# A four-layer graph attention stack: new start, new end and new ranks in the planned order

## Chip, cores and metric

The kernel runs on one core of one Trainium2 chip. The metric is the device time of one execution in microseconds, as a median of runs. Everything is in 32-bit floating point.

## What is computed

`x` has 128 graphs of 64 nodes with 512 features; `adj` is one 64 x 64 mask for each graph. Four pre-norm layers add to `x`; each one starts with `h = relu(layernorm(x))`.

```
layers 0, 2: q, k, v = h@Wq, h@Wk, h@Wv            # 4 heads of 64
             p = softmax(where(adj, q@k.T / 8, -max));   x += (p@v)@Wo + bo
layer 1:     g = layernorm(h)*gamma + beta;  q, k, v = g@Wqkv.T   # 8 heads of 64
             p = softmax(where(adj or eye, q@k.T / 8, -1e9));  x += (p@v)@w_out.T + b_out
layer 3:     m = h@map_w.T + map_b;  n = m / |m| by head          # 8 heads of 64
             q = m@q_w.T + q_b;  k = m@k_w.T + k_b
             p = softmax(where(mask, -1e10, q@k.T / 8)) * keep
             a = (n@n.T > 0.1) * p
             x += relu((a @ (h@gcn_map_w.T + gcn_map_b)) @ gcn_W.T / (sum(a) + 1))
```

## The kernel before

The 8192 rows of `x` are cut into 16 groups of 512 rows, which are four blocks of 128, two graphs to a block. The names used below are `(l, s)` for layer and group. A group goes through a layer in these steps: load (`loads`), layer norm (`layernorms`, one stream for each half of 256 rows), transposition of the tokens (`transposes`), projections (`projections`), scores and softmax (`front`), transposition of the probabilities (`turns`), and PV, output projection and residual (`attention`; `last` in layer 3).

**Products.** A projection is a 2 x 2 block product. `winograd` does it with seven half-size products instead of eight, into banks named `mA`, `mB` and `mC`. It needs sums of the weights (`sums_of_a`, once for each weight) and of the transposed tokens (`sums_of_b`, four for each operand, into a tile `t` and, for the third, in place). GpSimd makes most of these sums; for group 0 of layer 0 VectorE makes them. ScalarE and VectorE then take the results out of the banks. V of layers 0 and 2 has half the width. Scores, PV and the last transposes are 64 x 64 matmuls.

**Transposition of the tokens.** The first groups of layers 0 and 2 go through TensorE (`ptr`, L672), each block of 128 rows evicted by one ScalarE copy (L676). The others of these layers are moved by 16 DMAs of 32 rows each (`moves`, L630) into `F`, and VectorE then transposes 32 x 32 blocks (L645). In layers 1 and 3 ScalarE and GpSimd make the moves.

**The order of the work.** The order on every engine is written out by a planner in the kernel (`Order`): each stream of work is a generator that yields operations with an assumed cost (`pe(0.432)`, `act(0.6)`, `load(3.9)`). At each step the planner issues the operation that can start first by its own clock; among equals the lower rank wins. The table `RANK` gives a rank for each kind of stream and layer. Evictions have rank 0 and may go ahead of others on ScalarE and VectorE. On the chip each engine then runs its list in this order and waits where it must. SyncE (SP) issues nearly all DMAs, also in this order.

**The start.** SP issues four loads of one block each for group 0. ScalarE issues the first weights, Wq and Wk of layer 0, in four parts, and then the two loads of group 1. SP goes on with the mask, Wv and Wo. `x` has two buffers (`r_xin`).

**The end.** In layer 3 the residual rows of two blocks are loaded into one of three buffers (`r_xres`, L1279), VectorE adds the clamped PV to it (`finish`, L1293), and SP stores it (L1298). The softmax of layer 3 is multiplied by the neighbour mask, its sums are made, and `divide` divides by them on GpSimd (L1080). The last group's probabilities are transposed by TensorE (`by_tensor`, L1106), not by copies. `add_rows` (L954) adds a bias row to V on GpSimd, four instructions a group, after V has been evicted.

Of the kernel before, what the change touches and what calls it, by code (L numbers as in the profile page):

```python
# [14 lines left out]
P = 128  # L15
D = 512
N = 64
TB = 4
NC = D // P
# [11 lines left out]

RANK = {
    "load": (6.5, 0.3, 3, 3.5),
    "norm0": (4.5, 5.5, 6, 5.5),
    "norm1": (4.5, 6, 5, 6),
    "move": (6.5, 6.5, 2, 6.5),
    "turn": (3, 1.5, 4.5, 3.5),
    "part": (4, 1.5, 5, 5),
    "weight": (0.3, 6.5, 0.3, 3),
    "proj": (3.5, 5, 5, 6),  # L40
    "out": (1.5, 5, 5, 0.3),
    "front": (2, 3.5, 0.5, 4),
    "soft": (0.3, 3, 1, 4.5),
    "near": (3, 0.5, 6, 4),
    "trans": (4, 3.5, 3, 2.5),
    "att": (2.5, 2.5, 2, 6),
    "res": (2.5, 2.5, 4.5, 4.5),
    "msum": (1, 4, 1, 1),
    "length": (5, 5, 0.3, 5),
# [195 lines left out]
def gnn_stack(ctx: ExitStack, tc: tile.TileContext, a: dict, out: bass.AP):  # L245
# [109 lines left out]
    first_w, first_t, begun_w, loads_begun = (od.event() for _ in range(4))  # L355
    bo, bo_done = {}, {}

    def sums_of_a(A, vector=False):

        for o, i0, i1, op in ((4, 2, 3, ALU.add), (5, 4, 0, ALU.subtract),  # L360
                              (6, 1, 5, ALU.subtract), (2, 0, 2, ALU.subtract)):
            if vector:
                yield dve(0.75)
                nc.vector.tensor_tensor(A[:, o], A[:, i0], A[:, i1], op)
            else:
                yield pool(0.0026 * A.shape[2] * A.shape[3])
                nc.gpsimd.tensor_tensor(A[:, o], A[:, i0], A[:, i1], op)

    def sums_of_b(B, T, made, vector=False):

        for i, o, i0, i1 in ((0, T[0], B(0, 1), B(0, 0)), (1, T[1], B(1, 1), T[0]),
                             (2, T[2], B(1, 1), B(0, 1)), (3, T[3], B(1, 0), T[1])):
            if vector:
# [5 lines left out]
            if i:  # L379
                made[i].set()  # L380

# [3 lines left out]
    def weights():  # L385
        for key, parts in units:
# [5 lines left out]
            first = key == "qk0"  # L392
            for src, dst in parts(t):
# [8 lines left out]
            if first:  # L402
                begun_w.set()
                yield ("wait", 0.0, 5.0)
                first_w.set()
                yield ("wait", 0.0, 2.5)
                yield loads_begun
# [17 lines left out]
            yield from sums_of_a(t, key == "qk0")  # L425
            w_sums[key].set()

# [42 lines left out]
    def scales(v, there=None):  # L470

        mv = small.tile([P, 2, 2], F32, tag="mv", name="mv")
        for t in range(2):
# [4 lines left out]
            nc.vector.bn_stats(st, v[:, t, :])  # L478
            yield dve(0.17)
# [41 lines left out]
    def loads(steps):  # L521
        for l, s in steps:
# [3 lines left out]
            for half in range(2):  # L526
# [5 lines left out]
                if (l, s) == (0, 1):  # L532
                    if half == 0:
                        yield begun_w
                    yield ("act", 0.5, 0.0)
                elif (l, s) == (0, 0):
# [11 lines left out]
                (nc.scalar if (l, s) == (0, 1) else nc.sync).dma_start(  # L548
                    v, x_of(l, s)[half * H:(half + 1) * H, :].rearrange("(t p) d -> p t d", p=P))
                if (l, s) == (0, 1):  # L550
                    if half == 1:
                        loads_begun.set()
                    yield ("wait", 0.0, 8.0)
# [4 lines left out]
    def layernorms(steps, half):  # L558

        for l, s in steps:  # L560
            yield rank(f"norm{half}", l) if (l, s) != (0, 0) else Rank(0.3)
# [3 lines left out]
            rs = yield from scales(x, first_x[2 * half:] if (l, s) == (0, 0) else None)  # L565
# [84 lines left out]
    def transposes(steps):  # L650

        for l, s in steps:
            yield rank("turn", l) if (l, s) != (0, 0) else Rank(0.3)
# [9 lines left out]
            for half in range(0 if (l, s) in turned + by_dma else 2):  # L663
                yield n_ready[l, s, half]
                x, xe = normed[l, s]
                for t in range(2):
                    b = 2 * half + t
                    pt, pe_ = yield from r_mm.new("ptr")
                    pt = pt.rearrange("p (c n) -> p c n", c=NC)
                    for c in range(NC):  # L670
                        yield pe(0.115)
                        nc.tensor.transpose(pt[:, c, :], x[:, b, c * P:(c + 1) * P], ident)  # L672
                    if b == TB - 1:
                        xe.set()
                    yield act(0.6)
                    nc.scalar.copy(h[:, :, b * P:(b + 1) * P], pt)  # L676
                    pe_.set()
                if (l, s, half) == (0, 0, 0):
                    yield from has_h(l, s, h)
            if (l, s) != (0, 0) and (l, s) not in turned:  # L680
                yield from has_h(l, s, h)
            yield from sums_of_b(quarters(h), *hB[l, s][1:], (l, s) == (0, 0))
            if (l, s) == (0, 0):
                first_t.set()

    def has_h(l, s, h):
        T, t_done[l, s] = yield from r_t.new("T")
        hB[l, s] = (quarters(h), with_room(T, quarters(h)), made())
# [822 lines left out]
```

## Time and profile before

| | us |
|---|---|
| median of 3 runs | 2678.46 (2673.72 to 2681.55) |
| profiled execution | 2677.01 |
| its span | 2675.2 |
| TensorE busy in it | 2630.3 |
| VectorE, ScalarE, GpSimd busy | 1853.5, 1889.7, 1591.0 |
| granted TensorE clock, mean | 0.998 |

The table of busy times tells which engine has no room left. The table by stage divides the span and shows where TensorE is idle. The list of waits tells for what. The timeline shows the instructions in order of time, with start, duration, and in brackets the idle time before with what ended it. Times of one profiled execution are used throughout; they are spans from the first instruction to the last, so the execution's own time is a little longer.

### The profile page before, as it was taken

The numbers are of one execution on the slowest core, as the hardware profiler recorded it, in microseconds if no ns is written. First come the engines' busy times: TensorE is split into PE (matmuls) and PEld (weight loads), VectorE is DVE, ScalarE is ACT, GpSimd is POOL, SyncE is SP. The second block draws the span as 40 slices with busy tenths as digits, with TensorE's granted clock in tenths as the row PEclk, the third lists the DMA queues.
The fourth block names the chain that finished last, engine by engine and source line by source line (L and its number), as shares of the span: only waits on it lengthen the run. The fifth ranks groups of instructions, "written<-read, shape, count | busy, mean of one in ns | idle before, by whom it ended". The sixth has DMA issues, their size and how long they took to land.

```text
span 2675.2 us, 63987 instructions
## 1 busy us (share of the span) xinstructions
PE 2630.3 (98%) x26344; PEld 2308.6 (86%) x26344; DVE 1853.5 (69%) x2842; ACT 1889.7 (71%) x3517; POOL 1591.0 (59%) x1248
## 2 busy tenths in 40 slices
PE   7999999999999999999999999999999999999998
PEld 6888888888888888888899999988888888888887
DVE  6777676677667766766667777757676667776566
ACT  5676767888887788787567777776667766677653
POOL 4776776645444543545666767786556555556553
PEclk9999999999999999999999999999999999999999
DMA  5665663212111211114556666422322232222222
GB/s 155 165 178 141 171 150 129 85 65 80 49 49 65 80 49 59 68 66 104 138 155 155 166 151 170 141 76 81 94 66 66 81 101 78 66 65 70 68 82 59
DMA packets 413940, 270.02 MB, mean 101 GB/s; under 512 B 277456, under 2 KB 322512, under 8 KB 413648
## 3 DMA queue, kind: packets, MB, share of 16 engines
q1 hardware_dynamic: 401440, 253.35, 34.3%
q10 hardware_dynamic: 12208, 12.58, 1.4%
q8 instruction: 207, 3.39, 0.5%
q14 instruction: 85, 0.70, 0.1%
HBM read 166.77 MB, written 67.63 MB: 88 GB/s over the span
## 4 chain that ended last, share of the span: by engine, by line
PE 91%; DMA 2%; DVE 2%; SPq 2%; ACT 1%; issue 1%; POOL 1%; DVEq 0%; ACTq 0%; POOLq 0%
PE mA L714 47%; PE mC L714 23%; PE mB L714 12%; PE sc L1038 3%; PE po L1240 2%; PE cos L1038 1%; PE po L1410 1%; SPq L630 1%; PE mmn L981 1%; DMA F<-xin 1%; DMA w_vo<-in_Wv 0%; ACT E L1060 0%; SPq L548 0%; DMA adj<-in_adj 0%; DMA w_k<-in_Wk 0%
## 5 line engine op out<-in xcount | busy, mean ns | idle before, releaser
L1177 POOL TENSOR_TENSOR xres<-xres,u 128x512 f32<-128x512 f32 x192 | 247.5, 1295 | 415.7 <-ACT u L1172 389.6
L1089 ACT COPY F<-E 32x512 f32<-32x512 f32 x752 | 462.6, 615 | 23.3 <-POOL E L1080 12.4
L494 ACT ACTIVATE xin<-xin,rs 128x512 f32<-128x512 f32 x320 | 244.1, 808 | 36.0 <-DMA F<-xin 18.4
L1156 POOL TENSOR_TENSOR xres<-xres,u 128x512 f32<-128x512 f32 x192 | 252.9, 1335 | 25.6 <-DMA xres<-in_x 13.8
L594 ACT COPY hT<-xin 32x512 f32<-32x512 f32 x390 | 240.1, 616 | 7.2
L478 DVE BATCH_NORM_STATS2 st<-xin 128x6 f32<-128x512 f32 x320 | 213.8, 668 | 29.5 <-DMA xin<-in_x 19.4
L731 ACT COPY v<-mA 128x256 f32<-128x256 f32 (+1 forms) x192 | 92.1, 479 | 136.5 <-PE mA L714 133.4
L378 POOL TENSOR_TENSOR t<-hT,t 128x512 f32<-128x512 f32 x126 | 184.4, 1463 | 4.8 <-issue 1.5
L485 POOL TENSOR_TENSOR rs<-rs,mhalf 128x2 f32<-128x2 f32 x160 | 117.4, 737 | 71.8 <-DVE rs L483 48.2
L1074 DVE TENSOR_REDUCE sm<-E 128x16 f32<-128x1024 f32 x124 | 150.1, 1211 | 9.1 <-ACT E L1060 4.6
L714 PE MATMUL mA<-w_vo,t 128*128 128x128 f32 (+1 forms) x768 | 141.3, 316 | 4.1 <-ACT v L731 2.6
L378 POOL TENSOR_TENSOR t<-hT 128x512 f32<-128x512 f32 x63 | 92.9, 1475 | 79.7 <-DVE hT L604 54.8
L1080 POOL TENSOR_TENSOR E<-E,sm 128x1024 f32<-128x1024 f32 x64 | 122.0, 1916 | 25.9 <-DVE sm L1078 21.1
L1172 ACT COPY u<-mA 128x512 f32<-128x512 f32 x144 | 84.3, 586 | 74.2 <-PE mA L714 71.6
L714 PE MATMUL mA<-hT,w_qk 128*128 128x256 f32 x512 | 132.5, 385 | 4.3 <-ACT v L731 4.2
L731 ACT COPY qk<-mA 128x512 f32<-128x512 f32 x96 | 56.2, 585 | 111.2 <-PE mA L714 107.9
L591 POOL COPY hT<-xin 32x512 f32<-32x512 f32 x90 | 55.7, 618 | 131.3 <-ACT xin L494 128.8
L714 PEld LDWEIGHTS mA<-w_vo,t 128*128 128x128 f32 x768 | 115.0, 192 | 15.9 <-ACT v L731 2.8
L1093 DVE STREAM_TRANSPOSE F<-F 128x1024 f32<-128x1024 f32 x94 | 116.0, 1234 | 17.6 <-ACT F L1089 17.6
L954 POOL TENSOR_TENSOR v<-v,gcn_row 128x512 f32<-128x512 f32 x64 | 80.8, 1294 | 79.0 <-ACT v L731 79.0
L714 PE MATMUL mA<-t,w_qk 128*128 128x256 f32 x512 | 121.7, 380 | 5.5 <-POOL t L378 3.2
L1060 ACT ACTIVATE E<-sc,mx 128x64 f32<-128x64 f32 x512 | 122.4, 329 | 4.2 <-DVE mx L1057 4.2
(231 smaller groups left out, 7310.9 us busy)
## 6 DMA issues: line engine op xcount, KB each, us to landing
x<-xres SPq DMA_DIRECT2D x96, 512.0 KB
xin<-x SPq DMA_DIRECT2D x96, 512.0 KB
xres<-x SPq DMA_DIRECT2D x64, 512.0 KB
F<-xin SPq DMA_DIRECT2D x480, 64.0 KB
xres<-in_x SPq DMA_DIRECT2D x32, 512.0 KB
u<-rs SPq DMA_DIRECT2D x128, 128.0 KB
xres<-x SPq DMA_DIRECT2D x64, 256.0 KB
out<-xres SPq DMA_DIRECT2D x64, 256.0 KB
```

The costliest lines, as they stand in the source:

```text
L378: nc.gpsimd.tensor_tensor(o, i0, i1, ALU.subtract)
L478: nc.vector.bn_stats(st, v[:, t, :])
L494: nc.scalar.activation(v[:, t, :], v[:, t, :], func, bias=rs[:, 2, t:t + 1], scale=rs[:, 0, t:t + 1])
L594: nc.scalar.copy(o, v)
L714: nc.tensor.matmul(o, l, r, start=(first and m == 0 and k == 0), stop=(k == KC - 1), skip_group_check=True)
L731: nc.scalar.copy(o, p3)
L1060: nc.scalar.activation(E[:, i, :], S3[:, i, :], AF.Exp, bias=mx[:, i:i + 1], scale=0.125)
L1074: nc.vector.tensor_reduce(o, E, AX.X, ALU.add)
L1080: nc.gpsimd.tensor_mul(E, E, sm[:, :, None].to_broadcast([P, 16, N]))
L1089: nc.scalar.copy(F[g * N + 32 * k:g * N + 32 * (k + 1), :, 32 * i:32 * (i + 1)], E[g * N + 32 * i:g * N + 32 * (i + 1), :, 32 * k:32 * (k ...
L1156: nc.gpsimd.tensor_add(xr[:, t, :], xr[:, t, :], bo[l])
L1177: nc.gpsimd.tensor_add(v, v, both(u))
```

## The change

- **Start.** SP issues group 1's loads, ahead of Wv and Wo. VectorE writes a few elements into the buffers of both, once the statistics of group 0's last block have been issued, and the loads wait for these writes. `LEAD` names groups 0 and 1, and a rank `lead` holds for their layer norm and transposes. Two blocks of transposes share one bank pair and one ScalarE copy of twice the size (`from_bank`); this holds wherever TensorE transposes.
- **Group 0's Q and K.** `school` takes eight plain products instead of the seven of `winograd`: four with the first half of the tokens, four with the second. They need no sums. The sums of Q's and K's weights, which group 1 uses, are made once group 0 has been transposed; its own tokens' sums are still made, for V, the two that matter here (T[2] in place, and A[2] of the weights) only after the last of the eight products has read its operand.
- **End.** For the last group `divide` does its multiplication on VectorE. `finish` is started before PV and takes each of its two blocks as soon as that block's PV is done; in the last group it stores each block by itself, with half as many rows to a store and twice as many stores.
- **Ranks.** All ranks are new, and the planner's cost of one transpose step of the last group is 0.52 instead of 0.25.

```diff
+LEAD = [(0, 0), (0, 1)]
 RANK = {
-    "load": (6.5, 0.3, 3, 3.5),
-    "norm0": (4.5, 5.5, 6, 5.5),
-    "norm1": (4.5, 6, 5, 6),
-    "move": (6.5, 6.5, 2, 6.5),
...
-    "att": (2.5, 2.5, 2, 6),
-    "res": (2.5, 2.5, 4.5, 4.5),
...
+    "lead": (0.3, 1.5, 5.5, 5),
+    "load": (4, 5.5, 1.5, 2),
+    "norm0": (1.5, 3.5, 3.5, 6.5),
+    "norm1": (4.5, 2.5, 1, 4),
+    "move": (6.5, 4.5, 6, 0.3),
...
+    "att": (2.5, 0.5, 2, 2),
+    "res": (5.5, 6, 1.5, 5.5),
...
@@ def weights():
+            if key == "vo0":
+                yield x_there
+                yield dve(0.06)
+                nc.vector.memset(t.rearrange("p a k n -> p (a k n)")[:, 0:11 * H:2 * H], 0.0)
...
-                yield loads_begun
...
+            if first:
+                od.spawn(first_sums(t), rank("weight", 0))
+                continue
...
+    def first_sums(t):
+        yield h_whole
+        yield from sums_of_a(t, True)
+        w_sums["qk0"].set()
@@ def scales(v, there=None):
             nc.vector.bn_stats(st, v[:, t, :])
+            if there and there[t] is first_x[-1]:
+                x_there.set()
@@ def loads(steps):
-                if (l, s) == (0, 1):
-                    if half == 0:
-                        yield begun_w
-                    yield ("act", 0.5, 0.0)
+                if (l, s) == (0, 1) and half == 0:
+                    yield x_there
+                    yield dve(0.06)
+                    nc.vector.memset(x[:, :, 0:1], 0.0)
...
-                (nc.scalar if (l, s) == (0, 1) else nc.sync).dma_start(
+                nc.sync.dma_start(
@@ def transposes(steps):
-                for t in range(2):
-                    b = 2 * half + t
-                    pt, pe_ = yield from r_mm.new("ptr")
+                pt, pe_ = yield from r_sc.new("ptr")
...
+                od.spawn(from_bank(h[:, :, half * H:(half + 1) * H].rearrange(
+                    "p c (t n) -> p t c n", t=2), pt, pe_, copied), 0)
...
+    def from_bank(o, p_, pe_, done):
+        yield act(1.06)
+        nc.scalar.copy(o, p_)
+        pe_.set()
+        done.set()
...
+    def school(A, B, out_, used, begun, whole):
+        every = []
+        for k in range(2):
+            if k:
+                yield whole
+            room = []
+            for i in range(2):
+                room.append((yield from (r_mm if i else r_ma).new("mP")))
+            for j in range(2):
+                for i in range(2):
+                    yield from product(room[i][0], A[:, 2 * i + j], B(j, k), False, j == 0)
+                    if j:
+                        read, done = od.event(), od.event()
+                        od.spawn(out_.first(i, k, room[i][0], read, done), 0)
+                        od.spawn(when([read], room[i][1]), 0)
+                        every.append(done)
+                if k and not j:
+                    half_used.set()
+        begun.set()
+        od.spawn(when(every, used), 0)
@@
-    def divide(E, sm):
+    def divide(E, sm, vector=False):
...
-        yield pool(1.95)
-        nc.gpsimd.tensor_mul(E, E, sm[:, :, None].to_broadcast([P, 16, N]))
+        if vector:
+            yield dve(1.22)
+        else:
+            yield pool(1.95)
+        (nc.vector if vector else nc.gpsimd).tensor_mul(E, E, sm[:, :, None].to_broadcast([P, 16, N]))
@@ def by_tensor(E, e):
-                yield quads(0.25)
+                yield quads(0.52)
@@
-    def finish(s, u, po, poe, got):
+    def finish(s, u, po, poe, got, halves):
...
+            yield halves[b]
...
+            if s == NG - 1:
+                for s2 in range(2):
+                    yield load(2.8)
+                    q = slice(s2 * H, (s2 + 1) * H)
+                    o = out[(s * TB + 2 * u + b) * P:(s * TB + 2 * u + b + 1) * P, q]
+                    nc.sync.dma_start(o.rearrange("(i n) e -> n i e", n=N),
+                                      v[s2 * N:(s2 + 1) * N])
```

## The prediction

> **What bounds the kernel now.** I read the busy table first, then the table by stage, then who waited for whom, then the timeline at both ends.
>
> ```profile
> PE 2630.3 (98%) x26344; PEld 2308.6 (86%) x26344; DVE 1853.5 (69%) x2842; ACT 1889.7 (71%) x3517; POOL 1591.0 (59%) x1248
> ...
> 0.00:20.00 20.00, 8.60 (x29) 6.85 (x30) 9.68 (x33) 6.71 (x10) 6.67 (x15) 1.00 0.75 228
> 20.00:50.00 30.00, 24.52 (x206) 21.81 (x205) 19.75 (x45) 18.95 (x44) 10.24 (x11) 1.00 0.32 110
> 50.00:100.00 50.00, 46.10 (x483) 39.89 (x482) 35.04 (x52) 28.90 (x60) 40.69 (x33) 0.97 0.75 177
> 100.00:700.00 600.00, 592.93 (x5738) 528.82 (x5738) 426.81 (x722) 450.50 (x886) 377.48 (x308) 1.00 0.45 120
> 700.00:1350.00 650.00, 648.06 (x5855) 568.60 (x5853) 444.86 (x671) 487.91 (x766) 332.42 (x276) 1.00 0.26 78
> ```
>
> TensorE is busy for 2630.3 of 2675.2 us; nothing that leaves its work alone can win more than the other 45. The first two numbers of a stage are its length and PE's busy time. Of the 45 idle us, 11.4 lie in the first 20, 5.5 in the next 30, 3.9 in the next 50, 7.1 up to 700; all of 700 to 2660 has 6.3, and the last stretch after 2660 has 10.8. So there are three places to win: the start, layer 0, the tail.
>
> ```profile
> PE ptr L672 <- ACT xin L494: 11.3, 2, 8.9
> PE mA L714 <- ACT v L731: 7.8, 9, 2.6
> PE mA L714 <- DVE t L375: 3.2, 4, 2.3
> PE mA L714 <- POOL t L378: 3.2, 1, 3.2
> ```
>
> These waits (total, times, longest) name them: layer norm before the first transposes, evictions of V in layer 0, and the operand sums of groups 0 and 1. The timeline of the start and of the tail, start and duration first:
>
> ```profile
> 11.51 0.41 ACTq L548 DMA_DIRECT2D xin<-in_x  x1
> 11.95 0.58 ACT L676 COPY hT<-ptr 128x512 f32<-128x512 f32 x1 [2.43 <-DMA w_vo<-in_Wv]
> 14.48 2.93 PE L714 MATMUL mA<-hT,w_qk 128*128 128x256 f32 x6
> ...
> 2655.91 4.95 POOL L954 TENSOR_TENSOR v<-v,gcn_row 128x512 f32<-128x512 f32 x4 [5.12 <-ACT v L731]
> 2660.82 1.89 POOL L1080 TENSOR_TENSOR xin<-xin,f 128x1024 f32<-128x1024 f32 x1
> 2663.07 1.26 SPq L1279 DMA_DIRECT2D xres<-x  x2
> 2668.86 1.29 DVE L1293 SCALAR_TENSOR_TENSOR xres<-po,xres 128x512 f32<-128x512 f32 x2 [3.61 <-DMA xres<-x]
> ```
>
> ScalarE's first eviction of a transpose stands behind its own issue of group 1's second load. At the end the last residual load can go only when a store has freed its buffer, and the last VectorE step waits for that load.
>
> A third reading uses the start times of the mB product of each group's Q and K. In layer 2 it recurs every 26.62 us (1399.51, 1426.13, 1452.74); in layer 0 12 groups from 107.76 to 437.67 take 27.49 each. The work is the same. I add it from rows: a full product 1.73 x 7, V's product 0.89 x 7, the output's 0.86 x 7, scores and PV 1.01 each, four changes of tile size at 0.1: 26.8, so layer 2 runs without stalls and layer 0 loses 0.88 a group.
>
> **What the Trainium skill says.** "TensorE: Matmul & The Clock Gate", Part 1: the array runs at half clock until some 3.4 us of sustained work. The trace agrees: the 6 matmuls at 14.48 take 2.93 us where 8 take 1.89 later, and the rate is full from about 18.5. "DMA: Bandwidth & Descriptors", Anatomy of one DMA: a semaphore wait happens on the issuing sequencer, not in the DMA engine. The trace agrees: ACT had ended at 9.53 and stood until 11.51 with the issue at L548. The first page also has ScalarE and VectorE as strict FIFO (Architectural detail); the DVE load wait below bears it out, since everything behind it stood.
>
> **The change part by part.** The comparison is with the profiled execution's own 2677.0 us (span 2675.2 and 1.8 around it); the median of the runs shown, 2678.5, is 1.5 above it, so I add 1.5 at the end.
>
> *Start.* Group 1's two loads leave ACT's queue; SP issues them, and Wv and Wo, only after VectorE's memsets at about 9.4. Two memsets are added, 0.1 each by the row at 0.84. Eviction: transposes of blocks 0 and 1 end near 10.4, then one copy of two blocks (1.06 by the row of L1109, where two took 0.58 each). The first product starts at about 11.6 instead of 14.48. It is cold: 3.5; two cold transposes 1.6; so 16.7, then seven warm products 12.1 and one pair of group 1's transposes 0.9: Q and K end at 29.7. Before they ended at 33.0. This includes the eighth product, +1.73, which is paid; in return no product waits for T on VectorE (2.3) or for an eviction of its own bank. V and scores take 8.2 as before, so group 1 starts at about 37.9 (41.3 before). Its third product needs POOL's sums of group 1: their source is evicted by about 32.5, two sums at 1.3 end near 35, PE asks at 41.3, so the 3.15 wait goes. What is late next: group 2's transposed input, by 16 moves behind the layer norm at about 41.4, 0.85 each, some 2.5 to land and 2.5 on VectorE: 61 against a PE that could ask at 60. At 61 PE has done 46.7 us of work; before, at 74.0, it had done 49.2 and 1.73 less was due. So 74.0 - 61 - (49.2 - 46.7) - 1.73 = 8.8 net. The added wait: behind x_there on SP stand adj, bo, the vectors and group 2's loads; 2 MB at the 228 GB/s of the first stage are 8.8 us, so Wv lands near 19 to 20 and POOL's sums of it end by 26, where V wants them past 30. If the held loads took 10 us more, that cover would be gone and the gain with it. Bounds: -11 to -3; I take -8.8.
>
> *Layer 0 by the new ranks.* The order of instructions shows a pattern that repeats each group: V's seven products in a row, PV and output among the next group's Q and K. I walk one group with the durations above, S the end of scores. PV to S+1.0, three matmuls of mC to S+2.3, the PV copy (1.02) S+1.2 to 2.3: met. Exponentials in five bursts end at S+9.2, sum, reciprocal and POOL's division at S+13.2; the three F copies then run to S+15.1, the V eviction (0.37) to S+15.5, and PE wants its bank at S+15.8. The other V evictions are ready 0.2 to 0.8 early. The next hT is written by S+32.9 for S+33.3. SP: 16 moves at 0.75 to 0.85 end near S+24, plus 2.5 to land, for VectorE at S+30. So no stall, 26.8 a group; POOL has 19.4 of it. If all holds, 14 groups at 0.88 give 12. Margins of 0.2 to 0.4 us will not all hold; I take -7, bounds -13 to +4.
>
> *Layers 1 to 3 by the ranks.* PE's order is the same word for word over most of layer 1, and little changed in layers 2 and 3, which have almost nothing to win. The planner's costs are the old ones but for one, 0.52 for a group of the last transposes, which is what the trace has (64 in 2.08, in four groups). Its plans kept PE at 99.7% here from 700 on. A miss costs: +1.5, bounds -4 to +8.
>
> *Tail.* The division moves to VectorE: E times a factor at 1.23 (the L1374 row at 2651.05; the one at 2644.45 took 2.12) for POOL's 1.90, and the second one no longer stands behind 4.95 of row additions. PV of group 14 goes ahead of the last two V products, so its stores go 3.3 us earlier, the last residual load lands at 2665.4 instead of 2668.7. But these PV (2.1) and a transpose (2.1) now stand ahead of V's last product: its eviction, and POOL's four additions behind it, end 4 us later, at 2665. The last PV ends at 2665.5 (2667.1 before), the last half on VectorE at 2667.5 (2670.2). SP then issues eight stores of half the size instead of four, 0.6 each; its queue ends near 2670, 1.4 before the old end. I take -2, bounds -5 to +1.
>
> Sum: -8.8 - 7 + 1.5 - 2 = -16.3; 2677.0 - 16.3 + 1.5 = 2662.
>
> **Rivals.** *Only the ends win:* layer 0's stalls are placed anew, not removed. For it: every margin found is under half a microsecond. Against it: layer 2's pattern has no stall at all with the same work. -8.8 - 2 + 1.5: 2669. *The held loads come late:* VectorE's queue has two statistics of group 1 ahead of the sums of group 0's operands; were those loads to land 5 us later than the 14 to 16 reckoned, V of group 0 stands, and the start gains 3: with half of layer 0, 2672. Against it: before, such a load took 5 us with more traffic. *Slower: POOL or the moves become layer 0's clock.* In the new order SP's stores wait for POOL's last addition of the group, and the next half load and residual stand behind them; moves of the next group follow. The chain has 26.8 us and I find some 4 us of slack. If an issue takes 1.1 us instead of 0.75 to 0.95, 16 cost 4 to 5 more, the slack is gone, and each 0.1 beyond costs 1.6 a group: at 1.2, 1.6 in each of 14 groups, +22 in place of -7: 2692. Against it: issues in the stages shown are 0.6 to 0.95. *The change does less than it says:* the memsets could fail to hold the loads; but the SP instruction waits for a VectorE semaphore, so it holds.
>
> **How the numbers follow.** The forecast 0.55, only the ends 0.21, late loads 0.12, the slower case 0.12. A measurement of this kernel can tell about 0.3%, 8 us, from no change: faster is below 2670.5. The forecast's own range is 2653 to 2670; the first rival falls below 2670.5 for the most part. Faster 0.74, within 0.14, slower 0.12. With the bounds of the terms the range is 2652 to 2680; it leaves out the slower case and little else.
>
> **What would show it.** The first Q and K product at 11 to 12 us and Q and K done by 30; no wait of group 1 for POOL's sums; mB of Q and K in layer 0 every 26.7 to 27.0 us; layer 2 still at 26.6; the last residual load landed by 2666 counted on the old clock, the end 4 to 8 us after the last PV. Wrong would be a layer-0 spacing of 27.5 or more, V of group 0 waiting for a DMA, or new waits of over 1 us in layers 1 to 3.

## Result and the profile after

The changed kernel takes 2678.01 us (median of 13 runs, 2674.79 to 2685.52); the kernel before, on the same chip, 2678.3 (13 runs). The ratio is 1.0004, 95% interval 0.9995 to 1.0014: no difference, where 2662 was forecast.

The busy table of the changed kernel, then its table by stage (stage, length, PE's busy time, then PEld, VectorE, ScalarE, GpSimd):

```profile
PE 2629.7 (98%) x26352; PEld 2308.0 (86%) x26352; DVE 1918.9 (72%) x2843; ACT 1890.3 (71%) x3508; POOL 1608.8 (60%) x1246
```

```profile
0.00:20.00 20.00, 10.08 (x37) 8.50 (x38) 8.27 (x32) 6.24 (x7) 2.12 (x8) 1.00 0.73 240
20.00:50.00 30.00, 29.92 (x233) 27.02 (x232) 25.01 (x51) 21.17 (x45) 21.59 (x21) 1.00 0.41 125
50.00:100.00 50.00, 46.86 (x499) 42.16 (x498) 35.92 (x55) 31.94 (x71) 38.44 (x31) 0.97 0.69 162
100.00:700.00 600.00, 597.49 (x5769) 532.07 (x5768) 465.56 (x732) 455.95 (x882) 383.57 (x315) 1.00 0.45 123
700.00:1350.00 650.00, 648.36 (x5941) 569.06 (x5940) 459.44 (x676) 487.79 (x785) 322.00 (x275) 1.00 0.26 78
1350.00:2000.00 650.00, 647.09 (x6407) 574.74 (x6406) 461.02 (x713) 459.67 (x947) 463.22 (x344) 1.00 0.46 122
2000.00:2500.00 500.00, 487.38 (x5441) 416.14 (x5440) 350.84 (x456) 337.94 (x613) 298.09 (x209) 1.00 0.30 76
```

The kernel before has, in its last two of these stages:

```profile
1350.00:2000.00 650.00, 649.52 (x6499) 575.26 (x6498) 465.10 (x717) 455.39 (x955) 446.11 (x344) 1.00 0.46 125
2000.00:2500.00 500.00, 497.25 (x5417) 427.35 (x5418) 340.95 (x471) 350.59 (x634) 294.39 (x213) 1.00 0.27 76
```

TensorE's idle time is length minus busy, and the whole span then adds up:

| stage, us | idle before | idle after | difference |
|---|---|---|---|
| 0 to 100 | 20.8 | 13.1 | -7.7 |
| 100 to 700 | 7.1 | 2.5 | -4.6 |
| 700 to 1350 | 1.9 | 1.6 | -0.3 |
| 1350 to 2000 | 0.5 | 2.9 | +2.4 |
| 2000 to 2500 | 2.7 | 12.6 | +9.9 |
| 2500 to the end | 11.9 | 10.5 | -1.4 |
| PE busy, all | 2630.3 | 2629.7 | -0.6 |
| span | 2675.2 | 2673.0 | -2.2 |

The start and layer 0 win 12.3 us of idle time, and the stages from 1350 to 2500, which end in layer 3, give 12.3 back.

Idle time is only part of it, since the same work can keep TensorE busy for longer or shorter. A better measure is a point at which both kernels have the same work left: the mB product of Q and K of the fourth group of layer 2. From there to the end, before and then after:

```profile
1399.51:2675.20 1275.69, 1260.57 (x13569) 1097.45 (x13567) 886.88 (x1273) 863.72 (x1673) 792.06 (x584) 1.00 0.35 97
1382.97:2673.00 1290.03, 1263.98 (x13569) 1099.01 (x13567) 904.17 (x1274) 866.10 (x1671) 816.95 (x581) 1.00 0.37 96
```

The same 13569 matmuls are left. Up to this point the changed kernel is 16.5 us ahead, its eighth product paid; from here on it loses 14.3. TensorE's waits in the changed kernel (total, times, longest) say what for:

```profile
PE po L1475 <- DVE xres L1349: 13.1, 16, 0.8
PE ptr L688 <- ACT xin L515: 8.8, 1, 8.8
PE mC L741 <- ACT m L762: 5.3, 6, 1.7
```

The first and third lines are new; both lie in layer 3. The first is PV waiting for `finish` (L1349). The timeline around one such wait:

```profile
2183.01 1.04 PE L1475 MATMUL po<-v,F 64*64 64x64 f32 x56
2184.87 1.28 PE L1475 MATMUL po<-v,F 64*64 64x64 f32 x72 [0.81 <-DVE xres L1349]
```

and VectorE's instruction that falls into the gap:

```profile
2184.12 0.69 DVE L1349 SCALAR_TENSOR_TENSOR xres<-po,xres 128x512 f32<-128x512 f32 x1 [2.50 <-PE po L1475]
```

`finish` now reads the first block's half of a PV tile by itself, in every group of layer 3 and not only in the last. Each block has its columns in both of the tile's banks. The read is less early than the text of the change has it: the first block is done after four of the tile's eight PV steps, but VectorE starts at 2184.12, just after the seventh (56 of 64 matmul records), and the eighth step waits for VectorE. In group 0 it is after the fifth. Before, none did. TensorE stands 0.81 us: VectorE's 0.69 and the signal. There is one such wait in each of groups 0 to 13, none in group 14, and two in the last group.

The third line, the waits for m's eviction, was first put down to VectorE and GpSimd. Here are both engines in one group of layer 3 of the changed kernel:

```profile
2267.51 2.04 DVE L1437 TENSOR_TENSOR E<-E,Cf 128x1024 f32<-128x1024 f32 x1
2273.50 1.95 DVE L1437 TENSOR_TENSOR E<-E,Cf 128x1024 f32<-128x1024 f32 x1
```

```profile
2267.20 1.27 POOL L385 TENSOR_TENSOR mT_T<-m 128x512 f32<-128x512 f32 x1
2268.43 2.26 POOL L385 TENSOR_TENSOR t<-m,t 128x512 f32<-128x512 f32 x1
2272.47 1.90 POOL L1135 TENSOR_TENSOR E<-E,f 128x1024 f32<-128x1024 f32 x1 [1.78 <-DVE f L1130]
```

The product with the neighbour mask (L1437) starts while GpSimd is in an operand sum and ends 1.1 us after GpSimd has; GpSimd's next sum, queued behind, takes 2.26 instead of 1.27. The two take turns. The trace gives this with little scatter. Of the 30 products, the four that start with GpSimd idle take 1.22 us:

```profile
2613.10 1.22 DVE L1437 TENSOR_TENSOR E<-E,Cf 128x1024 f32<-128x1024 f32 x1
```

The other 26 start inside a GpSimd instruction with 0.25 to 0.97 us left to run, and each takes 1.22 us plus what is left, less 0.14. The groups by line of before, and then of after, give it over the layer (count, busy us, mean ns):

```profile
L1374 DVE TENSOR_TENSOR E<-E,Cf 128x1024 f32<-128x1024 f32 x30 | 39.3, 1309 | 0.6
```

```profile
L1437 DVE TENSOR_TENSOR E<-E,Cf 128x1024 f32<-128x1024 f32 x30 | 55.5, 1849 | 0.9
```

The planner's cost for this product is 1.22 us. With the old order that was nearly right; with the new ranks it is short by 0.6 on average. ScalarE has the exponential ahead of m's eviction in its list, and the exponential waits for VectorE. The timeline shows an eviction that TensorE waits for:

```profile
2316.73 1.06 ACT L1119 ACTIVATE E<-E 128x1024 f32<-128x1024 f32 x1 [2.43 <-DVE E L1116]
2317.69 0.82 ACT L762 ACTIVATE m<-mC,vecs 128x256 f32<-128x256 f32 x2
2318.57 1.99 PE L741 MATMUL mC<-hT,w_map 128*128 128x256 f32 x8 [1.69 <-ACT m L762]
```

VectorE's and TensorE's lines ahead of it show where the delay comes from:

```profile
2307.25 2.10 PE L1090 MATMUL sc<-kT,qT 64*64 64x64 f32 x128
2311.33 0.69 DVE L497 BATCH_NORM_STATS2 st<-xin 128x6 f32<-128x512 f32 x1 [4.03 <-DMA xin<-x]
2311.94 1.77 DVE L1100 COPY_PREDICATED sc<-adj,negs 128x1024 f32<-128x1024 uint8 x1
2315.48 1.22 DVE L1116 TENSOR_TENSOR E<-sc,mx 128x1024 f32<-128x1024 f32 x1
```

The scores are there by 2309.35. But VectorE's list has a statistics step of another group's layer norm directly ahead of their masking (L1100), and this step stands 4.03 us for its load. The masking then takes 1.77 us beside GpSimd's work, where it takes 1.22 with GpSimd idle. The product of the mask is not in this chain: the one before ended at 2275.45, and VectorE has had idle time since, the 4.03 us among it. All six waits for m's eviction have such a wait for a load ahead of them, of 2.6 to 4.0 us. In the kernel before, no statistics step stands directly ahead of the masking in this stretch.

**Theory** with which the runs were planned: start, layer 0 and tail win about what was reckoned; layer 3 loses it, in two separate ways: the early reads stop PV, and the new ranks bring VectorE's product beside GpSimd's work, which the plan does not know, so that VectorE is late. The wait for the load is a rival to the second half of this, and was not in the theory. **Rivals** named then: the gain at the start is only shifted, and any gap left open closes later whatever is done; the new ranks of layer 3 are simply worse; or the parts hang together so closely that no part has a price of its own.

### The profile page after: what moved, and what is told of

The parts are those of the page before. It is cut to its first block, busy times and chain, and to the rows that moved or that the text cites. A ratio compares the mean times of both kernels' runs of the same rounds, so it can differ in the third digit from the quotient of the medians.

```text
span 2673.0 us, 64016 instructions
## 1 busy us (share of the span) xinstructions
PE 2629.7 (98%) x26352; PEld 2308.0 (86%) x26352; DVE 1918.9 (72%) x2843; ACT 1890.3 (71%) x3508; POOL 1608.8 (60%) x1246
## 4 chain that ended last, share of the span: by engine, by line
PE 92%; DVE 3%; DMA 2%; issue 1%; SPq 1%; ACT 1%; POOL 1%; POOLq 0%; DVEq 0%
PE mA L741 47%; PE mC L741 24%; PE mB L741 12%; PE sc L1090 3%; PE po L1295 2%; DMA xin<-x 1%; PE cos L1090 1%; PE po L1475 1%; SPq L1361 1%; PE mmn L1033 1%; DVE xres L1349 1%; PE mP L741 1%; DVE sc L1100 0%; POOL v L1006 0%; PE ptr L688 0%
## 5 line engine op out<-in xcount | busy, mean ns | idle before, releaser
L515 ACT ACTIVATE xin<-xin,rs 128x512 f32<-128x512 f32 x320 | 248.8, 810 | 11.5 <-DVE rs L508 9.3
L385 POOL TENSOR_TENSOR t<-hT,t 128x512 f32<-128x512 f32 x126 | 178.4, 1416 | 4.8
L1135 POOL TENSOR_TENSOR E<-E,sm 128x1024 f32<-128x1024 f32 x64 | 122.5, 1920 | 61.3 <-DVE sm L1130 42.1
L385 POOL TENSOR_TENSOR t<-hT 128x512 f32<-128x512 f32 x63 | 82.9, 1316 | 123.7 <-DVE hT L621 111.6
L1100 DVE COPY_PREDICATED sc<-n,negs 128x1024 f32<-128x1024 uint8 x64 | 99.8, 1559 | 57.5 <-PE sc L1090 57.2
L741 PE MATMUL mA<-w_vo,t 128*128 128x128 f32 (+1 forms) x768 | 135.2, 312 | 1.5 <-ACT v L758 1.0
L741 PE MATMUL mA<-hT,w_qk 128*128 128x256 f32 x496 | 126.1, 382 | 3.3 <-DVE hT L662 3.1
L1135 POOL TENSOR_TENSOR E<-E,f 128x1024 f32<-128x1024 f32 x30 | 61.1, 2036 | 104.9 <-DVE nz L1180 57.2
L1106 DVE TENSOR_REDUCE mx<-sc 128x16 f32<-128x1024 f32 x96 | 116.9, 1218 | 2.5
```

The costliest lines, as they stand in the source:

```text
L385: nc.gpsimd.tensor_tensor(o, i0, i1, ALU.subtract)
L515: nc.scalar.activation(v[:, t, :], v[:, t, :], func, bias=rs[:, 2, t:t + 1], scale=rs[:, 0, t:t + 1])
L741: nc.tensor.matmul(o, l, r, start=(first and m == 0 and k == 0), stop=(k == KC - 1), skip_group_check=True)
L1135: (nc.vector if vector else nc.gpsimd).tensor_mul(E, E, sm[:, :, None].to_broadcast([P, 16, N]))
```

## Experiments

Ratios are to the kernel before on the same chip in the same series; 0.001 is 2.7 us. "Late finish" is the base of several others.

**Late finish.** In layer 3, all but the last group wait for both blocks, as before the change; ranks and the rest stay.

```diff
-            yield halves[b]
+            yield halves[b if s == NG - 1 else 1]
```

> The changed kernel with one edit: in every group but the last, finish waits for the PV of both blocks again, as before the change. Theory A (the early finish costs TensorE a wait of 0.81 us in each group of layer 3, because the last four PV matmuls of a tile were ordered behind VectorE's read of its first half): the 15 waits go, 15 x 0.81 = 12.2 us, so 2666 us, ratio to before 0.9955, and no PV wait on VectorE's xres is left before the last group. Theory B (the wait only shows where layer 3 is short anyway, and VectorE or the banks would hold TensorE elsewhere): the wait reappears at the next PV tile or at the cosines, 2674 to 2679 us, ratio 0.9985 to 1.0.

2668.1 us, ratio 0.9968 (0.9959 to 0.9976). TensorE's list of instructions differs from the changed kernel's in a few rows close together in layer 3 and nowhere else, so this is nearly the one edit alone. Its waits:

```profile
PE mC L741 <- ACT m L762: 11.1, 8, 2.9
PE po L1475 <- DVE xres L1349: 1.6, 2, 0.8
```

PV's waits fall from 13.1 us in 16 to 1.6 in 2, those of the last group. By the medians 9.6 of these 11.5 us arrive at the end, between the two times expected and nearer the first. The one trace of this kernel cannot confirm the sum: in it the waits for m's eviction go from 5.3 to 11.1, and it was taken of the slowest of 16 executions, the changed kernel's of the fastest of 13, so their spans are only 2.6 us apart. The rival that a gap closes later whatever is done falls.

**Half of the early reads** (groups 0, 2, ... 14 and the last):

```diff
-            yield halves[b if s == NG - 1 else 1]
+            yield halves[b if s % 2 == 0 or s == NG - 1 else 1]
```

> The late-finish kernel with VectorE's early read put back in every second group of layer 3 (groups 0, 2, ... 14 and the last), so half the dose. If each early read stops TensorE by its 0.8 us and nothing else is different, some 9 waits and 7.5 us of them return, and the time lies between the late finish (0.9968 of before) and the changed kernel (1.0004): 0.998 to 0.9995, about 2673 us on before's 2678. If what the late finish won came from some other place (a store or an eviction that happened to fall better), the time does not go by the count of waits: below 0.9975 or above 1.0005.

2670.35 us, 0.9979 (0.9973 to 0.9986); PV waits 7.4 us in 9. This is the cleanest of the runs: every engine's list of instructions is that of the changed kernel, instruction for instruction, and only the waits differ. Seven waits and 5.7 us of them are gone, m's waits are nearly the same (5.8 us against 5.3), and the ratio is 0.0025, 6.7 us, below the changed kernel's. The count and the waits are as expected. The ratio is 0.0001 outside the range that the expectation gave, with the interval across its lower end: against the late finish, where m's waits are 11.1, the time does not go by the count alone.

**Old ranks in layer 3** (the late finish, with layer 3's column of `RANK` as before the change):

```diff
-    "soft": (1.5, 1.5, 0.3, 1),
-    "near": (2, 2, 2, 2),
+    "soft": (1.5, 1.5, 0.3, 4.5),
+    "near": (2, 2, 2, 4),
...
```

> The previous kernel (late finish) with the ranks of layer 3 of before, those of layers 0 to 2 new. Theory A: the new layer-3 ranks put ScalarE's exponential ahead of the eviction of m (6 waits, 5.3 us); with the old ranks these go and layer 3 loses what it lost before: 4 to 5 us less than the previous kernel, 2661 us, ratio 0.9935. Theory B (the ranks of layer 3 are not the matter): within 1 us of the previous kernel.

2672.8 us, 0.9983 (0.9976 to 0.9991), where 2661 or the late finish's own time was expected. The waits for m's eviction are gone, no statistics step stands directly ahead of the masking, and TensorE idles 0.04 us between 2000 and 2500. But where layer 3 begins, inside a plan made for other ranks, PV waits twice:

```profile
PE po L1475 <- DVE E L1116: 9.6, 2, 6.0
```

The groups by line of this kernel:

```profile
L1437 DVE TENSOR_TENSOR E<-E,Cf 128x1024 f32<-128x1024 f32 x30 | 38.8, 1294 | 0.6
```

The instruction is the same and its operands are the same; with the old ranks it takes 1.29 us again, with the new 1.85. The ranks of layer 3 alone decide that. The new ones are not simply worse: the old ones lose 9.6 us at the seam.

**Cost of the mask product.** The late finish, with the last group's output whole too (see below), and the planner told what the product takes:

```diff
-        yield dve(1.22)
+        yield dve(2.0)
         nc.vector.tensor_mul(E, E, Cf.rearrange("p a (i k) -> p (a i) k", k=N))
```

> The kernel with the last output whole (0.9963 of before), where the planner is given 2.0 us, not 1.22, for the product with the neighbour mask (it takes 1.99 in the profile of layer 3). If TensorE's waits for m's eviction in layer 3 (13.3 us in 10) come from a VectorE that is later than its plan, they fall by 3 to 8 us and the ratio goes to 0.993 to 0.995. If another placement only puts the waits elsewhere, the ratio stays within 0.0015 of 0.9963.

2659.46 us, 0.9941 (0.9927 to 0.9954); the same kernel with the old cost has 0.9963 (0.995 to 0.9975), so the two intervals just touch. From the table by stage:

```profile
2000.00:2500.00 500.00, 500.00 (x5518) 429.09 (x5518) 374.30 (x474) 348.96 (x630) 310.15 (x213) 1.00 0.30 77
```

TensorE is never idle between 2000 and 2500, where the changed kernel lost 12.6 us. Groups by line:

```profile
L1437 DVE TENSOR_TENSOR E<-E,Cf 128x1024 f32<-128x1024 f32 x30 | 56.4, 1878 | 0.9
```

The product is as slow as ever, the masking is slower (1.80 us on average against 1.54 with the old cost), and neither costs TensorE anything between 2000 and 2500. What helped is another order on VectorE, ScalarE and GpSimd; TensorE's own list is the same but for one product near the end. With the old cost a statistics step stood directly ahead of the masking in ten groups between 1900 and 2520 and waited for its load each time, 35.9 us in all; here that is so in one, with 3.0 us. The masking now comes soon after the scores:

```profile
2074.26 1.50 DVE L1100 COPY_PREDICATED sc<-adj,negs 128x1024 f32<-128x1024 uint8 x1 [1.18 <-PE sc L1090]
```

The exponential behind it starts at 2079.97 us without a wait, where in the late finish one stood 3.65 us up to 2088.78, and the eviction of m is in time. So the waits for m's eviction came from the order of VectorE's list and the load in it, not from slow instructions in place. Whether it was the right cost that mattered, or whether any cost that moves the statistics step would do as well, no run here tells.

**Cost alone.** The changed kernel with the early reads kept and only the cost corrected, the fourth corner of the square:

> The changed kernel as it is, early reads in every group of layer 3, with the planner's cost of the product with the neighbour mask at 2.0 us instead of 1.22: the fourth case beside the changed kernel (neither), the late finish (1.0004 to 0.9968) and both together (0.9941, with the last output whole). If the two losses are separate, TensorE's waits for m's eviction in layer 3 go (5.3 us to under 2), its waits for VectorE's early reads stay near 13 in 16, and the ratio is 0.997 to 0.999 (5.3 us off 1.0004, or about what the cost won beside the late finish, 6 us, off it, with 1 us to either side). If one of them hides the other, it is either at 1.000 or more, or at 0.995 or less.

2673.31 us, 0.9989 (0.9981 to 0.9997). Its waits in layer 3 (1700 to 2500):

```profile
PE po L1475 <- DVE xres L1349: 9.8, 12, 0.9
PE mA L741 <- issue: 0.5, 1, 0.5
PE mC L741 <- ACT m L762: 0.5, 1, 0.5
```

| | early reads | late finish |
|---|---|---|
| product planned at 1.22 | 1.0004 | 0.9968 |
| planned at 2.0 | 0.9989 | 0.9941 (last output whole) |

Here too no statistics step but one stands directly ahead of the masking and waits. From 1.0004 the cost alone wins 0.0015, the late finish alone 0.0036, both 0.0063: separate losses, and additive within the intervals. The first of these is the least sure, since its interval just touches the changed kernel's (0.9995 to 1.0014). The cost alone brings 4 us and not 5.3; its new plan has a new wait of 3.2 us near the end, of the last transposes for the last division, and so has the version with both.

**A second cost,** 1.75 us instead of 1.5 for the predicated copy (L1100) in the layers with the wide exponentials, besides the first:

```diff
-        yield dve(1.5)
+        yield dve(1.5 if narrow else 1.75)
```

> As e13_cost_of_mask_product, and in the layers with the wide exponentials 1.75 us, not 1.5, for the predicated copy that masks the scores (1.74 in layer 3, up to 2.22). If a late VectorE is the cause, the waits for m's eviction fall below 5 us and the ratio is 0.992 to 0.9945. If the placement only moves the waits, it stays within 0.0015 of 0.9963, or is worse by the 1.4 us that its own plan is longer.

2658.45 us, 0.9936 (0.9924 to 0.9949): not to be told from the first cost alone. Waits for m's eviction are at 1.6 us in all, and nothing was left to win there. Both versions beat before and after.

**The tail's two parts.** The late finish with the last division on GpSimd:

```diff
-            od.spawn(neighbours(z, u, C, ce, nfv, found[u], s == NG - 1), rank("near", l))
+            od.spawn(neighbours(z, u, C, ce, nfv, found[u], False), rank("near", l))
```

> The late-finish kernel (2668.1 us, 0.9968 of before) with the last group's division put back on GpSimd. If the prediction's tail step is right, the division costs 1.90 instead of 1.23 and stands behind GpSimd's row additions, so the end comes 1 to 3 us later than with the late finish alone: 2669 to 2671. If another chain sets the end (the last residual load and the stores), it makes no difference: within 0.7 us of it.

2673.57 us, 0.998 (0.9974 to 0.9987), against 0.9968 (0.9959 to 0.9976) with it on VectorE. The centres are 3 us apart, at the upper end of what was expected; the two intervals just overlap. The traces place the difference: from the start of group 13's PV in layer 3, with 1290 matmuls left in both, this kernel takes 90.6 us to the end and the late finish 87.4.

The late finish with the last output whole, PV and stores not by halves:

```diff
-            yield halves[b if s == NG - 1 else 1]
+            yield halves[1]
-            if s == NG - 1:
+            if False:
...
-        for s2 in range(2 if s < NG - 1 else 0):
+        for s2 in range(2):
```

> The late-finish kernel with the last group's output also whole: VectorE reads after all 32 PV products, and one store of full size in place of two halves. If halves shorten the end (the prediction's tail), it is 0.5 to 2 us later than the late finish: 2668.6 to 2670. If halves only move the wait (the last two PV waits of 0.8 go, the last VectorE step and stores are longer), within 0.7 us of it, or earlier.

2667.51 us, 0.9963 (0.995 to 0.9975): no difference. From the same point its trace takes 86.5 us to the end. Halves do not shorten the end; their two waits of 0.81 us are in the late finish and not here.

**Group 0's Q and K by seven products** (late finish, without the eight plain ones):

```diff
+    half_used.set()
...
-                                       rank("proj", l), (l, s) == (0, 0))
+                                       rank("proj", l), False)
```

> The late-finish kernel with group 0's queries and keys by the seven products and their operand sums, as in every other group, instead of eight plain products. One product less is 1.73 us off TensorE. If the prediction's start is right, products then wait for VectorE's sums (2.3 us before) and for evictions of their bank, so it comes out 0 to 3 us slower than the late finish, with cumulative excess at 100 us up by 2 to 5. If the plain products only cost their 1.73, it is 1 to 2 us faster. If the later groups' planned order depends on the start, it differs by more than 4 us, most of it after 100 us.

2719.12 us, 1.0153 (1.0139 to 1.0168), the third case of the expectation and far beyond the first two. Within the first 100 us TensorE idles 22.6 us instead of 13.6. The timeline shows why:

```profile
16.29 1.89 PE L742 MATMUL mB<-hT,w_qk 128*128 128x256 f32 x8
26.49 3.68 PE L689 MATMUL ptr<-ident,xin 128*128 128x128 f32 x16 [8.31 <-ACT xin L516]
```

In this order group 1's transposes stand ahead of group 0's remaining products and wait for their layer norm, and ScalarE, which ends it, stands 6.7 us for VectorE. The other 40 us come later, in the order that the planner then writes for the later groups: 19.7 us are idle between 100 and 700 instead of 2.2, and over the whole run TensorE is busy for 2645.4 us instead of 2632.0, with a product less to do.

**Loads not held** (late finish, without the two memsets and the waits for them; the loads stay on SP):

```diff
-                if (l, s) == (0, 1) and half == 0:
-                    yield x_there
-                    yield dve(0.06)
-                    nc.vector.memset(x[:, :, 0:1], 0.0)
...
-            if key == "vo0":
-                yield x_there
-                yield dve(0.06)
-                nc.vector.memset(t.rearrange("p a k n -> p (a k n)")[:, 0:11 * H:2 * H], 0.0)
```

> The late-finish kernel without the wait that holds group 1's loads and Wv and Wo behind the first group's layer norm (the two small memsets go with it); they stay on the same queue. If holding them is what brings the first product to 11.9 us, the first blocks now land later beside that traffic, the first product starts 1 to 4 us later and the run is 1 to 4 us slower. If it is the move off ScalarE's queue that brings it, the start stays at 12 us and the time within 1 us.

2712.41 us, 1.0128 (1.0113 to 1.0144). At the start little is different: the first product comes at 12.13 us instead of 11.87, and the first 100 us have 15.7 us of idle time instead of 13.6.

```profile
12.13 3.78 PE L733 MATMUL mP<-hT,w_qk 128*128 128x256 f32 x8 [1.10 <-ACT hT L699]
```

So it is not the hold that brings the early start. What remains of the prediction's reason is the move off ScalarE's queue and the single copy of two blocks; this run does not part these two. Neither of the times expected was met. The loss comes later, in another order of the instructions: 22.0 us lie idle between 100 and 700, and TensorE is busy for 2644.1 us.

**Old ranks everywhere** (late finish; only `lead` stays new) and **new ranks alone** (the kernel before with the new table). The first edit, of which the second is the reverse in the kernel before:

```diff
-    "load": (4, 5.5, 1.5, 2),
-    "norm0": (1.5, 3.5, 3.5, 6.5),
+    "load": (6.5, 0.3, 3, 3.5),
+    "norm0": (4.5, 5.5, 6, 5.5),
...
```

> The late finish with all ranks of before (rank lead for groups 0 and 1 kept): start and end as changed. Theory A (start and ranks act separately, the start is worth 8 to 9 us, the new ranks 4 to 7 in layer 0): layer 0 has its mB spacing of about 27.5 us again and the time is 2667 to 2669 us, ratio 0.996. Theory B (the tight layer 0 comes from the start, which sets the phase of the groups, not from the ranks): spacing 26.6 us and about 2662 us, ratio 0.994.

> The kernel before with the new ranks and nothing else. Theory A (ranks alone: layer 0 gains 4 to 7, layer 3 loses about 5 by the waits for the eviction of m): 2675 to 2680 us, ratio 0.999 to 1.0005, with an mB spacing of 26.6 us in layer 0. Theory B (the spacing comes from the start): spacing 27.3 to 27.5 us, 2682 us, ratio 1.0015.

2683.2 us, 1.0028 (1.0021 to 1.0035), and 2735.51 us, 1.021 (1.0188 to 1.0232). None of the times expected was met, nor is the spacing of mB in layer 0 steady in either (22 to 43 us with the old ranks, 25 to 34 with the new ones alone). With the old ranks the new start loses 15.6 us between 100 and 700 and nearly nothing after. The new ranks on the old start idle in every stage, 27.0 us between 100 and 700 and 16.2 between 1350 and 2000; its longest entries:

```profile
PE mA L714 <- ACT v L731: 15.3, 12, 5.4
PE po L1240 <- DVE E L1064: 10.4, 1, 10.4
```

The third rival is right for start and ranks: they are one change. A rank table has no price without the start for which its plan was written, and leaving out two memsets at 10 us cost 43 us by the end.

## Why the prediction was wrong

**The step that failed is "Layers 1 to 3 by the ranks":** "PE's order is ... little changed in layers 2 and 3, which have almost nothing to win. ... A miss costs: +1.5, bounds -4 to +8". Between 1350 and 2500 the changed kernel has 12.3 us more idle time, and from the common point in layer 2 to the end it loses 14.3, beyond even that bound. The step looked at TensorE's order of work, and neither at the waits in it nor at VectorE's order. Two things were there.

- *The early reads were counted in the last group only.* The diff took away `finish`'s wait for the whole tile in all 16 groups, and the order of instructions had the new waits of PV in it. The 16 waits, 14 of them outside the last group, are 13.1 us. The run with half of the early reads, every list unchanged, shows it: seven waits fewer, 0.0025 less. The late finish gives 0.0036. The Trainium skill, "PSUM — Partial Sum Buffer", PSUM bank collisions raise a hardware error, says that a read must be kept by a semaphore from a matmul into the same bank, even at other columns, since the hardware doesn't stall there. The trace agrees in so far as TensorE stands behind a semaphore, 0.81 us each time, and VectorE's read of the first block starts only when the seventh of the tile's eight steps has ended (the fifth in group 0); whether the tile alone or the bank made the wait was not told apart, and by that page the wait alone could not be taken away without a race.
- *VectorE's order was taken over unread.* The new ranks of layer 3 put a statistics step, which waits for a load, directly ahead of the masking of the scores. It stands 2.6 to 4.0 us ahead of each of the six waits for m's eviction, 5.3 us in all. In the kernel with layer 3's old ranks and in those with the corrected cost, where this step stands elsewhere but for one group, these waits are 0.0 to 1.6 us. Which of layer 3's ranks does it, and whether the load comes late or the step was placed early, stays open.

A third thing was carried over too, and did not cost what the theory said. The prediction trusted the planner since "The planner's costs are the old ones" and its plans had kept PE at 99.7%. But a duration on VectorE holds only beside the same work on GpSimd. "SBUF — State Buffer", Who interferes with whom, has it: a VectorE instruction with two inputs in SBUF contends with a GpSimd instruction that reads SBUF, for ports of which the page says that they are an exclusive lock. The trace agrees: the product takes 1.31 us on average in the old order, 1.29 with the old ranks put back, 1.85 in the new, and GpSimd's sum behind it 2.26. The prediction even had the sign of it, in its two durations of the product in the last group, 1.23 and 2.12, and priced the tail with the short one; there it came true, at 1.22 (L1135 at 2658.24). No trace shows that this contention by itself made TensorE wait: with the product and the masking slower still, the run with the corrected cost has no idle time between 2000 and 2500.

**The rest, in its order.** *Start and layer 0:* reckoned -8.8 and -7, together -15.8; at the common point in layer 2 it is -16.5. The two terms were right in sum. To part them, count each matmul at its usual spacing in these traces (0.216 us for a 128x256 record, 0.112 for 128x128, 0.016 for 64x64): by this estimate the changed kernel is 8.3 us ahead at 100 us and 16.0 at 700, its eighth product paid. Idle time alone shows less (7.7 us, from which the product's 1.73 has still to be taken, and then 4.6), because in the kernel before TensorE also took longer over the same work. *Start:* the first product came at 11.89 us, Q and K ended near 30.4 (29.7 reckoned). The wait for POOL's sums of group 1 went. The next late item was the one named, group 2's input:

```profile
11.89 3.78 PE L741 MATMUL mP<-hT,w_qk 128*128 128x256 f32 x8 [1.10 <-ACT hT L707]
...
64.56 3.08 PE L741 MATMUL mA<-hT,w_qk 128*128 128x256 f32 x8 [3.14 <-DVE hT L662]
```

It came at 64.6, not 61, and TensorE asked at 61.4. Right in size; of its mechanism, the hold of the loads was not needed for the early first product, as the run with free loads showed. The load wait of VectorE that the prediction names as a sign of its strict order is plainest at 10.63 us of the kernel before: a statistics step stands 1.32 us for its load, and a step behind it (L487 at 11.24), whose input GpSimd had done at 10.09, stands too. *Layer 0:* the spacing of 26.7 to 27.0 that was asked for is 26.6 (145.28, 171.89, 198.49 us), so every margin held, and for that case 12 us had been reckoned. The 7 that was taken allowed for margins that would not hold. That 7.7 came of it is in part luck. Of the 10.6 us by which the 12 groups of before exceeded this rate, 5.1 were idle time; the rest lay in TensorE's busy time. *Tail:* reckoned -2; after 2500 the idle time fell by 1.4. The last PV ended at 2666.9 (2665.5 reckoned) and VectorE's last half at 2667.7:

```profile
2663.93 6.35 SPq L1356 DMA_DIRECT2D out<-xres  x8
...
2665.67 2.00 DVE L1349 SCALAR_TENSOR_TENSOR xres<-po,xres 128x512 f32<-128x512 f32 x3 [1.76 <-PE po L1475]
2666.41 0.49 PE L1475 MATMUL po<-v,F 64*64 64x64 f32 x8 [0.81 <-DVE xres L1349]
```

VectorE no longer waits for a residual load, and SP's queue ends at 2670.3, as reckoned near 2670. Beside the late finish the division on VectorE is worth 3.2 us to the end, and the halves cost 0.9 us. *The rivals:* the slower case, in which POOL or the moves become layer 0's clock, did not occur; layer 0 runs at its full rate. Of the three signs named as wrong, "new waits of over 1 us in layers 1 to 3" came true in the waits for m's eviction, up to 1.7 us. PV's waits of 0.81, which cost more, lay under that line sixteen times. The range of 2652 to 2680 is narrower than its terms: their bounds add up to 2645 to 2688.

With both losses mended, and the last output whole, the same change takes 2659.46 us, 0.9941 of before, in the neighbourhood of the forecast.

## What to carry to other kernels

An edit to a helper is priced by the number of its calls: count how many loops pass the line before following the one that the change is about, and look for short new waits that repeat, not for long ones. Follow a wait back past the engine that is named first: ScalarE waited for VectorE, and VectorE for a load in a step that had nothing to do with the scores. Where an order is planned from assumed durations, read them again in the new order (one product took 40% longer here), but look at what a corrected number does: here it won 0.0015 to 0.0022, and in the traces it did so by moving another step. And compare two kernels at a point where both have the same work left, since idle time alone showed 12.3 us of a lead of 16.5.

## What the runs showed of the hardware

A 128x1024 product of two SBUF operands on VectorE takes 1.22 us in the changed kernel when GpSimd is idle at its start. Begun inside a GpSimd instruction on large SBUF operands, it takes 1.22 us plus what is left of that instruction less 0.14 (26 of 30 products; the same sum holds for four of the 30 before). In the kernel before, ten began inside a GpSimd step on a 128x2 tile, with 0.31 to 0.34 us of it left, and were no longer. Over 30 products this made 16 us more on VectorE (39.3 to 55.5), and TensorE had no idle time between 2000 and 2500 in the kernel whose plan counted 2.0 us for each.

TensorE's busy time is no fixed sum of its work: with the same products, in the same order but for one, it was 2625.7 us with the cost corrected and 2630.2 with the old cost.
